# A gated cross-attention and FFN layer: the end of the kernel written in one planned order, with the work spread over engines anew

## The chip, the cores and the metric

The kernel runs on one core of one Trainium2 chip. The core has five engines, each of which works through its own list of instructions in order: TensorE (PE, matmuls), VectorE (DVE), ScalarE (ACT), GpSimd (POOL) and SyncE (SP, which here only issues DMAs). They wait for each other on semaphores. The metric is the device time of one execution in microseconds (us), the median of several; lower is better.

## The reference, cut to what matters

x has 32 batches of 224 tokens of 512 numbers, the context 32 batches of 750 keys of 384 numbers. All is float32.

```python
x = x + tanh(g_xattn) * attention(layernorm(x), ctx, mask, Wq, Wkv)   # 16 heads of 32
x = x + tanh(g_ffn) * ffn(layernorm(x))

def attention(x, y, pad_mask, Wq, Wkv):
    q, (k, v) = x @ Wq.T, split(y @ Wkv.T)
    a = where(pad_mask, (q * scale) @ k.T, -1e9)          # pad_mask is of the queries
    return softmax(a) @ v

def bitlinear(x, w, b):
    xq = act_quant(rmsnorm(x))        # 127 / max|row|, rounded to whole numbers, scaled back
    wq = weight_quant(w)              # w / mean|w|, rounded to -1, 0, 1, scaled back
    return xq @ wq.T + b
ffn = lambda x: bitlinear(gelu(bitlinear(x, w1, b1)), w2, b2)         # 512 -> 2048 -> 512
```

## The kernel before, in words

**Attention.** The main loop (line 915) runs over 128 steps, one for each batch `b` and each group `g` of four heads. In a step `weights` (369) makes, three times, the scores of 250 keys by 224 queries and four heads (`se`), lets ACT take the exponential into a tile `p`, and lets POOL add the two halves of `p` to `acc` (125 x 896; two adds, but for the first of the three, which takes one). There is one PSUM buffer for scores (`ps_s`, used by `sm` and `se` in turn), so PE fills it again only when ACT, or DVE, has emptied it. For the step after it, `maxima` (312) makes scores too (`sm`), which DVE reduces to row maxima (`mx`); `minus_max` splits these into three bfloat16 parts, `turn_max` (358) transposes them on PE and ACT copies the result to `nT`, the first operand of the next `se`. One step later come `values` (402, p by v, 24 matmuls into `po`), `sums` (416, four matmuls of ones by `acc` for the denominators, then a transpose and a reciprocal on DVE), `finish` (432, POOL multiplies) and `store` (441, four DMAs to `o_d` in DRAM).

A step is cut into six slots. Each has its fixed pieces, and what room is left for PE, ACT and DVE is filled by `Ffn.fill` (783).

**Weights.** In steps 0 to 10 the slots 1, 3 and 5 do not take FFN work but one of `weight_units` (451): the FFN weights are loaded twice, first for their mean, then in 16 pieces of 128 x 1024 for `quantise` (490), three passes of DVE over a piece (`wb`, `wb`, then the rounding into `w1q` or `w2q`, fp8).

**FFN.** It goes by pairs of 128 tokens; NF = 28 pairs. `ffn_units` (545) gives a pair's units: `load` (x into `xg`, the attention's result from `o_d` into `og`), `add`, `stats`, `rsqrt` (16 operations on two numbers a row), `norm`, `max`, three `sa`, `grid`, `bias`, `round`, `turn` (two DMA transposes into `xT`); then for each of the two tiles four `b` (4 matmuls `ph`, and DVE scales and adds the bias into `h`), `gelu`, `square`, two `hm` (row maxima), three `sb` (with a second rsqrt, `r3`), `cgrid` (a pass over `h`, 128 x 2048), `cround` (ACT, into `hq`), `cturn` (a DMA transpose into `hT`), two `c` (16 matmuls `po` with `w2q`; DVE adds into `xg`), and `out`. Passes over whole tiles are written for a fixed engine: `add`, `grid`, `bias` and `cgrid` on POOL, `norm`, `round` and `cround` on ACT. Operations on one or two numbers a row go to `small[0]`, which is POOL in the loop and DVE at the end.

Buffers order the units too: `Ffn.behind` (753) lists what a unit comes after. `xg` and `h` have two buffers, `og`, `xc`, `xq`, `xT` and `hq` one.

**What sets the order.** Everything is written through `Ordered` (44), which keeps the written order on each engine. `fill` takes the first ready unit that fits in a slot. `late` (814) gives PE more room, 0.3 us for each tile of backlog beyond `LATE` = 3, or beyond 1 in the last batches. The loop has one step more than there are attention steps, for the last `values`, `sums`, `finish` and `store`. What is left of the FFN is then written by `drain` (819): a list scheduler that takes, at each turn, the ready unit that could begin soonest (within 1.0 us), and among those the one with the longest rest of work behind it. It goes by the table `TAKES_US` (732), in which each unit has one engine.

Of the kernel before, what the change touches and what calls it, by code (L numbers as in the profile page):

```python
# [24 lines left out]
def flamingo_gated_layer(  # L25
# [343 lines left out]
    def weights(b, g, u):  # L369


        qT, kT, nT = q_of[b], k_of[b, g], nT_of[b, g]
        s = ps_s.tile([P, HG, 512], F32, tag="s", name=f"se_{b}_{g}_{u}")
        for j in range(HG):
            pe.matmul(
                s[:KC, j, : 2 * S].rearrange("p (i n) -> p i n", i=2),
                ones3[j * DH : j * DH + 3, :KC],
                nT[j * DH : j * DH + 3, :].unsqueeze(1).to_broadcast([3, 2, S]),
                start=True, stop=False,
            )  # L380
        for i in range(2):
            c = 2 * u + i
            for j in range(HG):
                rows = slice(j * DH, (j + 1) * DH)
                pe.matmul(
                    s[:KC, j, i * S : (i + 1) * S],
                    kT[rows, c * KC : (c + 1) * KC], qT[rows, g, :],
                    start=False, stop=(i == 1),
                )
        p = pp.tile([KC, HG, 2, S], F32, tag="p", name=f"p_{b}_{g}_{u}")  # L390
        act.activation(p.rearrange("p j i n -> p j (i n)"), s[:KC, :, : 2 * S], AF.Exp)
        p_of[b, g, u] = p
        if u == 0:
            acc_of[b, g] = accp.tile([KC, HG, S], F32, tag="acc", name=f"acc_{b}_{g}")
        acc = acc_of[b, g]
        if u == 0:
            gp.tensor_tensor(acc, p[:, :, 0, :], p[:, :, 1, :], ALU.add)
        else:
            for i in range(2):
                gp.tensor_tensor(acc, acc, p[:, :, i, :], ALU.add)  # L400
# [15 lines left out]
    def sums(b, g):  # L416

        po, acc = po_of[b, g], acc_of.pop((b, g))
        for j in range(HG):
            pe.matmul(  # L420
                po[j * DH : (j + 1) * DH, S : 2 * S], ones[:KC, :DH], acc[:, j, :],
                start=True, stop=True,
            )


        oT = op.tile([P, 2, S // DH, DH], F32, tag="oT", name=f"oT_{b}_{g}")
        dve.transpose(oT.rearrange("p a c d -> p (a c d)"), po[:, : 2 * S])
        rd = op.tile([P, S // DH], F32, tag="rd", name=f"rd_{b}_{g}")
        dve.reciprocal(rd, oT[:, 1, :, 0])
        po_of[b, g] = oT, rd  # L430
# [20 lines left out]
    def weight_units():  # L451
# [38 lines left out]
        def quantise(which, i):  # L490
            wl, to = held.pop(("wb", which, i))
            dve.tensor_scalar(wl, wl, wscale[:, which : which + 1], 1.0, ALU.mult, ALU.min)
            dve.tensor_scalar(wl, wl, -1.0, MAGIC, ALU.max, ALU.add)
            dve.tensor_scalar(to, wl, -MAGIC, None, ALU.add, saturate=False)
# [22 lines left out]

    NTI = NT // P
# [25 lines left out]

    def ffn_units(i):
# [6 lines left out]
        def a_load():  # L552
            s["xg"] = xgp.tile([P, TG, D], F32, tag="xg", name=f"xg_{i}")
            s["og"] = ogp.tile([P, TG, D], F32, tag="og", name=f"og_{i}")
            sp.dma_start(
                s["xg"],
                x.rearrange("b s d -> (b s) d")[rows, :].rearrange("(t p) d -> p t d", p=P),
            )
            sp.dma_start(s["og"], o_d[rows, :].rearrange("(t p) d -> p t d", p=P))

        def a_add():
            gp.tensor_tensor(s["xg"], s["xg"], s.pop("og"), ALU.add)
# [17 lines left out]
        def a_norm():  # L580
            s["xc"] = fp.tile([P, TG, D], F32, tag="xc", name=f"xc_{i}")
            for t in range(TG):
                act.activation(
                    s["xc"][:, t, :], s["xg"][:, t, :], AF.Identity, bias=s["nm"][:, t : t + 1]
                )
# [10 lines left out]
        def a_grid():  # L596
            for t in range(TG):
                gp.tensor_scalar(
# [4 lines left out]
        def a_bias():  # L603

            for t in range(TG):
                gp.tensor_tensor(s["xg"][:, t, :], s["xg"][:, t, :], b2g, ALU.add)

        def a_round():
            s["xq"] = fp.tile([P, TG, D], BF16, tag="xq", name=f"xq_{i}")
            act.activation(s["xq"], s["xc"], AF.Identity, bias=magic)  # L610

        def a_turn():
            s["xT"] = fp.tile([P, TG, NDC, P], BF16, tag="xT", name=f"xT_{i}")
# [3 lines left out]
        def b_matmul(t, f):  # L617
            if f == 0:
                s["h", t] = hp.tile([P, F], F32, tag="h", name=f"h_{i}_{t}")
# [14 lines left out]
        def b_gelu(t):  # L634
            h = s["h", t]
            act.activation(h, h, AF.Gelu)
            if small[0] is gp:

                act.activation(warm, magic, AF.Exp)
# [23 lines left out]
        def c_grid(t):  # L663
            h = s["h", t]
            gp.tensor_scalar(h, h, s[f"qb{t}"][0], MAGIC, ALU.mult, ALU.add)

        def c_round(t):
            s["hq", t] = fp.tile([P, F], BF16, tag="hq", name=f"hq_{i}_{t}")
            act.activation(s["hq", t], s.pop(("h", t)), AF.Identity, bias=magic)
# [15 lines left out]
        def c_store(t):  # L685
# [5 lines left out]
            ("add", 3, "load", 0, 0, 0, a_add),  # L691
            ("stats", 2, "add", 0, 0, 1.6, a_stats),
# [38 lines left out]
    ORDER_ONLY = "b", "c"  # L731
    TAKES_US = {
        "load": [("SP", 3.7)], "add": [("POOL", 2.5)], "stats": [("DVE", 1.7)], "rsqrt": [("DVE", 2.6)],
        "norm": [("ACT", 1.4)], "max": [("DVE", 1.2)], "sa0": [("DVE", 0.4)],
        "sa1": [("DVE", 0.2)], "sa2": [("DVE", 0.4)], "grid": [("POOL", 1.4)],
        "bias": [("POOL", 2.5)], "round": [("ACT", 1.2)], "turn": [("SP", 2.7)],
        "b": [("PE", 0.9), ("DVE", 0.75)], "gelu": [("ACT", 1.9)], "square": [("ACT", 2.1)],
        "hm": [("DVE", 1.2)], "sb0": [("DVE", 0.2), ("DVE", 1.8)], "sb1": [("DVE", 0.2)],
        "sb2": [("DVE", 0.4)], "cgrid": [("POOL", 2.0)], "cround": [("ACT", 2.0)],
        "cturn": [("SP", 2.3)], "c": [("PE", 1.75), ("DVE", 0.5)], "out": [("SP", 2.0)],  # L740
    }

    class Ffn:
# [9 lines left out]
        def behind(self, pair, name):  # L753
# [3 lines left out]
                "load": [(pair - XG, f"out{TG - 1}"), (pair - 1, "add")],  # L757
                "norm": [(pair - 1, "round")],
                "round": [(pair - 1, "turn")],
                "turn": [(pair - 1, f"b{TG - 1}3")],  # L760
            }
            if name[-1].isdigit():
# [3 lines left out]
                    f"b{t}0": [(pair, "turn"), (ph, f"cround{th}"), (p1, f"b{t1}3")],  # L766
                    f"square{t}": [(p1, f"square{t1}")],
                    f"sb{t}0": [(pair, f"hm{t}0"), (pair, f"hm{t}1"), (p1, f"sb{t1}2")],
                    f"cround{t}": [(p1, f"cturn{t1}")],
                    f"cturn{t}": [(ph, f"c{th}1")],  # L770
                    f"c{t}0": [(pair, "bias")],
                }
            return [at for at in before.get(name, []) if at[0] >= 0]

        def ready(self, pair, unit):
            name, lag, after = unit[:3]
            if after is not None:
# [36 lines left out]
        def late(self, stored, more):  # L814

            ready = stored * S // P - TG * self.next + sum(p[1][-1][0][:3] == "out" for p in self.parts)
            return 0.3 * max(0, ready - (LATE if stored < B - 3 else 1) - more)

        def drain(self):


            small[0] = dve
            free = dict.fromkeys(("PE", "ACT", "DVE", "POOL", "SP"), 0.0)
            end = {}

            def takes(name):
                kind = name.rstrip("0123456789")
                return TAKES_US.get(kind + name[-1]) or TAKES_US[kind]

            while self.next < NF:  # L830
# [4 lines left out]
            def rank(at):  # L835

                if at not in left:
                    left[at] = 0.0
                    left[at] = sum(us for _, us in takes(at[1])) + max(
# [7 lines left out]
            }  # L847
            while self.parts:
                self.slot += 10
                found = []  # L850
                for part in self.parts:
                    for unit in part[1]:
                        if self.ready(part[0], unit):
                            at = part[0], unit[0]
                            since = max(
                                [end.get(x, 0.0) for x in behind[at]
                                 if x[1].rstrip("0123456789") not in ORDER_ONLY
                                 or x[1][:-1] != at[1][:-1]], default=0.0,
                            )
                            since = max(since, free[takes(unit[0])[0][0]])  # L860
                            found.append((since, -rank(at), part, unit))
                soon = min(f[0] for f in found) + 1.0
                at, _, part, unit = min((f for f in found if f[0] <= soon), key=lambda f: f[1])
                part[1].remove(unit)
                self.at[part[0], unit[0]] = self.slot
                unit[6]()
                for engine, us in takes(unit[0]):
                    at = max(at, free[engine])
                    free[engine] = at + (0.1 if engine == "SP" else us)
                    at += us  # L870
                end[part[0], unit[0]] = at
# [43 lines left out]
    for n in range(N + 1):  # L915
        b, g = steps[n] if n < N else (B, 0)
        nxt = steps[n + 1] if n + 1 < N else None
# [16 lines left out]
        if n < N:  # L934
            put(0, 0.2, lambda: turn_max(n), first=True)
# [7 lines left out]
        if n < N and g == 2 and b + 2 < B:  # L943
# [5 lines left out]
        if n < N:  # L949
            put_values(4)  # L950
        if n < N and g < 2:
            put_values(3, 5)
        more = b + 1 < B and n < N
# [11 lines left out]
        for k in range(6):  # L965
            if k % 2 == 0:
                if nxt:
                    maxima(*nxt, k // 2)
            else:
                if k == 3 and last:  # L970
                    finish(*last)
                if n < N:
                    weights(b, g, k // 2)
            if k == 4 and nxt:
# [17 lines left out]
    ffn.drain()  # L992
# [38 lines left out]
```

## Time and profile before

| | us |
|---|---|
| three runs: median, lowest, highest | 3029.06, 3025.5, 3031.29 |
| the profiled execution, its own time | 3033.95 |
| its span, first to last instruction | 3032.1 |
| PE busy | 2898.3 |
| DVE, ACT, POOL busy | 1754.6, 1403.0, 2081.6 |
| mean granted clock of PE over the span | 0.986 of full |
| last exponential of the attention ends at | 2933.25 |

All times in the trace are from the start of the span. Every instruction is recorded by one helper, so all show line 52, and one goes by the names of tiles: `se` and `sm` are scores, `pk`, `pv` and `pq` projections, `po<-p,v` the attention's values, `ph` and `po<-w2q` the two FFN products. "PE" is matmuls, "PEld" weight loads. A line of the waits reads: who waited, for whom, total us, times, longest.

### The profile page before, as it was taken

The numbers are of one execution on the slowest core, as the hardware profiler recorded it, in microseconds if no ns is written. First come the engines' busy times: TensorE is split into PE (matmuls) and PEld (weight loads), VectorE is DVE, ScalarE is ACT, GpSimd is POOL, SyncE is SP. The second block draws the span as 40 slices with busy tenths as digits, with TensorE's granted clock in tenths as the row PEclk, the third lists the DMA queues.
The fourth block names the chain that finished last, engine by engine and source line by source line (L and its number), as shares of the span: only waits on it lengthen the run. The fifth ranks groups of instructions, "written<-read, shape, count | busy, mean of one in ns | idle before, by whom it ended". The sixth has DMA issues, their size and how long they took to land.

```text
span 3032.1 us, 62700 instructions
## 1 busy us (share of the span) xinstructions
PE 2898.3 (96%) x26774; PEld 1839.4 (61%) x26774; DVE 1754.6 (58%) x2641; ACT 1403.0 (46%) x1396; POOL 2081.6 (69%) x2675
## 2 busy tenths in 40 slices
PE   8998999999999999999999999999999999999964
PEld 4655566566666666666666666666666666666632
DVE  4577565555656556555556556565565555555535
ACT  2332354454545445354354545444543554544543
POOL 3465867768667777776676777766767777767762
PEclk9999999999999999999999999999999999999977
DMA  4333222123222223222222321223222122322112
GB/s 141 93 111 98 52 50 55 48 55 74 59 66 38 63 59 74 66 56 48 51 54 61 73 67 35 63 57 72 56 60 66 28 71 61 73 68 51 25 44 66
DMA packets 352696, 190.02 MB, mean 63 GB/s; under 512 B 282144, under 2 KB 305056, under 8 KB 352288
## 3 DMA queue, kind: packets, MB, share of 16 engines
q1 hardware_dynamic: 352416, 186.01, 25.2%
q8 instruction: 209, 3.42, 0.5%
q14 instruction: 71, 0.58, 0.1%
HBM read 119.86 MB, written 29.39 MB: 49 GB/s over the span
## 4 chain that ended last, share of the span: by engine, by line
PE 79%; ACT 8%; DVE 6%; POOL 4%; DMA 2%; issue 1%; SPq 0%; ACTq 0%; POOLq 0%; DVEq 0%
PE po L52 17%; PE se L52 13%; PE pk L52 13%; PE sm L52 12%; PE pv_None L52 11%; PE ph L52 6%; ACT p L52 6%; DVE mx L52 4%; PE pv L52 4%; PE pq L52 3%; POOL acc L52 2%; POOL h L52 1%; ACT L52 1%; ACT h L52 1%; DMA hT<-hq 1%
## 5 line engine op out<-in xcount | busy, mean ns | idle before, releaser
L52 POOL TENSOR_TENSOR acc<-acc,p 125x896 f32<-125x896 f32 x512 | 1073.2, 2096 | 296.0 <-ACT p L52 274.4
L52 DVE TENSOR_REDUCE mx<-sm 112x4 f32<-112x2000 f32 (+1 forms) x384 | 860.9, 2242 | 597.9 <-PE sm L52 597.6
L52 ACT ACTIVATE p<-se 125x1792 f32<-125x1792 f32 x384 | 639.1, 1664 | 717.7 <-PE se L52 711.3
L52 PE MATMUL pk<-y,wkv_sb 128*128 128x375 f32 x1536 | 545.1, 491 | 9.8 <-DMA y<-in_ctxT 9.8
L52 PE MATMUL sm<-kT,qT 32*112 32x500 f32 (+1 forms) x4096 | 427.2, 509 | 27.3 <-ACT p L52 17.7
L52 POOL TENSOR_TENSOR acc<-p 125x896 f32<-125x896 f32 x128 | 268.5, 2098 | 247.3 <-ACT p L52 247.3
L52 PEld LDWEIGHTS pk<-y,wkv_sb 128*128 128x128 f32 x1536 | 277.7, 191 | 179.6 <-issue 43.2
L52 PE MATMUL pv_None<-wkv_sb,y 128*125 128x256 f32 x1548 | 367.9, 387 | 0.0
L52 PE MATMUL se<-qT,kT 32*125 32x224 f32 x6144 | 360.2, 349 | 0.0
L52 PEld LDWEIGHTS pv_None<-wkv_sb,y 128*125 128x125 f32 x1548 | 280.1, 187 | 130.7 <-issue 88.3
L52 PE MATMUL po<-p,v 125*32 125x224 f32 x6144 | 319.2, 356 | 0.0
L52 PEld LDWEIGHTS se<-qT,kT 32*125 32x125 f32 x6144 | 295.9, 183 | 0.0
L52 PEld LDWEIGHTS sm<-kT,qT 32*112 32x112 f32 x4096 | 159.5, 171 | 186.1 <-ACT p L52 120.8
L52 ACT COPY kT<-pk 128x375 f32<-128x375 f32 x256 | 120.1, 469 | 318.0 <-PE pk L52 317.6
L52 DVE SCALAR_TENSOR_TENSOR h<-ph,qa_am,b_sb 128x512 f32<-128x512 f32 x224 | 165.3, 747 | 169.3 <-PE ph L52 147.1
L52 PEld LDWEIGHTS po<-p,v 125*32 125x32 f32 x6144 | 187.2, 110 | 119.9 <-issue 44.4
L52 PE MATMUL ph<-w1q,xT 128*128 128x512 fp8e4 x896 | 227.5, 388 | 23.2 <-DMA xT<-xq 22.9
L52 PE MATMUL po<-w2q,hT 128*128 128x256 fp8e4 x1792 | 219.5, 277 | 26.1 <-DMA hT<-hq 26.1
L52 PE MATMUL pq<-xTb,wq_sb 128*128 128x224 f32 x1024 | 221.1, 359 | 1.1 <-DVE wq_sb L52 0.7
L52 PEld LDWEIGHTS <-hT 128*128 128x128 bf16 x1792 | 170.7, 99 | 68.5 <-DMA hT<-hq 28.0
L52 PEld LDWEIGHTS pq<-xTb,wq_sb 128*128 128x128 f32 x1024 | 186.9, 190 | 25.4 <-issue 16.9
L52 POOL TENSOR_TENSOR yo<-oT,rd 128x224 f32<-128x224 f32 x128 | 73.7, 576 | 184.3 <-DVE rd L52 117.9
(119 smaller groups left out, 2914.3 us busy)
## 6 DMA issues: line engine op xcount, KB each, us to landing
y<-in_ctxT SPq DMA_DIRECT2D x31, 1125.0 KB, 6.9
x<-in_x SPq DMA_DIRECT2D x32, 448.0 KB, 7.7
xTb<-in_xT SPq DMA_DIRECT2D x32, 448.0 KB, 3.9
o_d<-yo SPq DMA_DIRECT2D x512, 28.0 KB, 1.6
xg<-in_x SPq DMA_DIRECT2D x28, 512.0 KB, 3.7
og<-o_d SPq DMA_DIRECT2D x28, 512.0 KB, 4.6
out<-xg SPq DMA_DIRECT2D x56, 256.0 KB, 2.1
wa<-in_w1T SPq DMA_DIRECT2D x8, 512.0 KB, 7.3
```

The lines of the kernel that those rows point to most:

```text
L52: return lambda *args, **kw: tc.keep_in_program_order(build(*args, **kw))
```

## The change

- **Last step.** The loop's extra step goes, and the last step is no longer in the loop either. Its `turn_max`, three `weights`, and the last two steps' `values` and `sums`, `finish` and `store` are handed to `drain` as units beside the FFN's. A `gelu` in the drain comes after the last `weights`. In the last step POOL no longer adds the two halves of the last third into `acc`; PE sums them with eight more matmuls of ones.
- **Engines.** In the drain a unit may have several ways in `TAKES_US` (`add`, `grid`, `bias` and `cgrid` on POOL or DVE, `norm`, `round` and `cround` on ACT or DVE, the small operations on DVE or POOL); the planner takes the way that ends first, with 1 us added for each us of DVE. `small[0]` is set for each unit. SP's entries have the time of their queue apart, and the window is 2 us.
- **Homes.** The last two pairs have no tiles of their own kind: x and the attention's result go into a `y` tile, `xc` and `xq` into a `v` tile, `xT` into a `kT` tile, `hq` into `x` tiles, and the hidden tiles of the last pair but one into the projection weights `wq_sb` and `wkv_sb`. Their entries in `behind` shrink accordingly. The last pair loads x at once, and fetches the attention's result after the last `store`.
- **Held back.** `late` takes 3 in the last batches, where it took 1 (and the bounds of "last" move).
- **Weights.** The third pass of `quantise` goes from DVE to ACT.

```diff
-        else:
+        elif (b, g, u) != (*steps[-1], 2):
             for i in range(2):
                 gp.tensor_tensor(acc, acc, p[:, :, i, :], ALU.add)
...
+        parts = [acc]
+        if (b, g) == steps[-1]:
+            parts += [p_of[b, g, 2][:, :, i, :] for i in range(2)]
+        for i, part in enumerate(parts):
+            for j in range(HG):
+                pe.matmul(
+                    po[j * DH : (j + 1) * DH, S : 2 * S], ones[:KC, :DH], part[:, j, :],
+                    start=(i == 0), stop=(i == len(parts) - 1),
+                )
...
-            dve.tensor_scalar(to, wl, -MAGIC, None, ALU.add, saturate=False)
+            act.activation(to, wl, AF.Identity, bias=magic, saturate=False)
...
+    def rounded(to, of):
+        if small[0] is dve:
+            dve.tensor_scalar(to, of, -MAGIC, None, ALU.add)
+        else:
+            act.activation(to, of, AF.Identity, bias=magic)
...
+            if i >= NF - 2:
+                both = yp.tile([P, NYC * M], F32, tag="y", name=f"xo_{i}")
+                both = both[:, : 2 * TG * D].rearrange("p (a t d) -> p a t d", a=2, t=TG)
+                s["xg"], s["og"] = both[:, 0], both[:, 1]
...
-            gp.tensor_tensor(s["xg"], s["xg"], s.pop("og"), ALU.add)
+            small[0].tensor_tensor(s["xg"], s["xg"], s.pop("og"), ALU.add)
...
-            gp.tensor_scalar(h, h, s[f"qb{t}"][0], MAGIC, ALU.mult, ALU.add)
+            small[0].tensor_scalar(h, h, s[f"qb{t}"][0], MAGIC, ALU.mult, ALU.add)
...
-            return 0.3 * max(0, ready - (LATE if stored < B - 3 else 1) - more)
+            return 0.3 * max(0, ready - (LATE if stored < B - 8 else 3) - more)
...
-            small[0] = dve
-            free = dict.fromkeys(("PE", "ACT", "DVE", "POOL", "SP"), 0.0)
+            draining.append(True)
+            free = {"PE": 0.0, "ACT": 0.0, "DVE": 4.3, "POOL": 5.0, "SP": 0.0}
...
+                            way = min(
+                                takes(unit[0]), key=lambda way: course(at, way)[1]
+                                + 1.0 * sum(us for engine, us in way if engine == "DVE"),
                             )
...
+                small[0] = {"DVE": dve, "POOL": gp}.get(way[-1][0], act)
                 unit[6]()
...
-    ffn.drain()
+    last = steps[-2:]
+    ffn.drain(
+        [("top", 0, None, 0, 0, 0, lambda: turn_max(N - 1))]
+        + [(f"w{u}", 0, None, 0, 0, 0, lambda u=u: weights(*last[1], u)) for u in range(3)]
+        + [
+            (name, 0, None, 0, 0, 0, lambda do=do, at=at: [f(*at) for f in do])
+            for name, at, *do in (
+                ("val", last[0], values, sums), ("fin0", last[0], finish), ("sto0", last[0], store),
+                ("vlast", last[1], values, sums), ("fin1", last[1], finish), ("sto1", last[1], store),
+            )
+        ]
+    )
```

## The prediction

> **What bounds the kernel now.** I read the page first, then five windows over the end, then the chain of waits and the totals of waits there, then the stretch in which the weights are quantised.
>
> ```profile
> PE 2898.3 (96%) x26774; PEld 1839.4 (61%) x26774; DVE 1754.6 (58%) x2641; ACT 1403.0 (46%) x1396; POOL 2081.6 (69%) x2675
> PE   8998999999999999999999999999999999999964
> PEclk9999999999999999999999999999999999999977
> ```
>
> TensorE is busy in 96% of the span, at a granted clock of nine tenths or more, except at both ends. In the middle only taking TensorE work away helps; what else can be won lies in the first slices and in the last two.
>
> ```profile
> 2846.00:2899.00 53.00, 49.16 (x458) 29.38 (x460) 25.93 (x37) 20.13 (x22) 36.88 (x37) 0.94 0.22 51
> 2899.00:2933.00 34.00, 21.01 (x266) 12.01 (x258) 17.04 (x28) 24.99 (x20) 26.23 (x46) 0.85 0.03 6
> 2933.00:2960.00 27.00, 14.42 (x120) 10.00 (x120) 4.15 (x9) 3.48 (x4) 13.95 (x17) 0.69 0.31 67
> 2960.00:2996.00 36.00, 15.46 (x54) 6.24 (x55) 23.33 (x71) 14.52 (x12) 12.57 (x10) 0.67 0.25 59
> 2996.00:3032.10 36.10, 19.00 (x141) 13.99 (x138) 16.87 (x45) 13.72 (x9) 4.54 (x3) 0.85 0.31 73
> ```
>
> Columns: stretch, length, busy time of PE, weight loads, DVE, ACT, POOL, then clock, DMA share, GB/s. The last exponential ends at 2933.25 (call this instant E). From E to the end, 98.9 us, PE works 48.9, DVE 44.4, ACT 31.7 and POOL 31.1: no engine is the bound; they take turns. The chain shows why:
>
> ```profile
> 2945.12 2.01 ACT hq L52
> 2947.15 4.27 DMA hT<-hq
> 2951.46 6.24 PE po L52 x32
> 2957.73 0.48 DVE xg L52
> 2958.21 0.09 DVE qa_c L52
> ...
> 2961.83 4.21 DMA xT<-xq
> 2966.09 5.75 PE ph L52 x16
> ```
>
> One tile is rounded, turned and multiplied before DVE gets to the reciprocal of the next pair, since that stands behind `xg<-po` in DVE's order. The totals from 2899 on say the same of DVE, and show one hole before E:
>
> ```profile
> DVE xg L52 <- PE po L52: 34.2, 11, 9.9
> ...
> PE se L52 <- ACT nT L52: 6.4, 1, 6.4
> ```
>
> The last pair's rsqrt starts only at E+39.4 (2972.62), its last transposed input lands at E+56.5 (2989.7), the last transposed hidden tile at E+91.7 (3024.95).
>
> **Part 1, the rounding of the weights (16 passes, DVE to ACT).** DVE's timeline of that stretch, and what PE waits for from 175 to 300:
>
> ```profile
> 198.18 2.46 DVE L52 TENSOR_SCALAR wb<-wb 128x1024 f32<-128x1024 f32 x1
> 200.67 2.58 DVE L52 TENSOR_SCALAR w1q<-wb 128x1024 fp8e4<-128x1024 f32 x1
> ...
> 213.84 0.69 DVE L52 TENSOR_SCALAR wb<-wb 128x1024 f32<-128x1024 f32 x1
> 214.57 0.70 DVE L52 TENSOR_SCALAR w1q<-wb 128x1024 fp8e4<-128x1024 f32 x1
> ```
> ```profile
> PE se L52 <- DVE mx L52: 9.9, 11, 3.6
> ```
>
> The same pass takes 0.69 us alone and 2.46 to 2.58 where a POOL `acc` runs beside it. Taking the third pass away gives DVE 5 x 2.55 + 11 x 0.70 = 20.4 us, but PE can gain only what it waited for: the gain lies between 0 and 9.9. By single holes of PE in front of `se`: four of 0.77 behind the slow passes go (3.1), one of 1.92 behind a 2.45 third pass goes nearly whole (1.8), one of 3.54 is a wait for a weight load and shrinks by the pass of 0.70. Sum 5.6. ACT takes 16 passes; the nearest row is `xq`, 128x1024, 1.15 us, 18.4 in all, and ACT is busy 4 to 5 us in 15 here. Each stands just behind an exponential, and behind it a copy of `kT` or `v`. If instead each delayed an exponential by its 1.15, PE would lose up to 18; I take 5.6 as gain.
>
> **Part 2, work held back.** The instruction order shows that behind the last exponential 24 groups of `ph` and 14 of `po` with `w2q` now stand, where 16 and 12 stood. A group of four `ph` takes PE 0.865 us from start to start, one of sixteen `po` 1.75. So 8 x 0.865 + 2 x 1.75 = 10.4 us leave the stretch where PE is the bound. The hole of 6.4, a gelu with two table loads (1.28 each) ahead of `nT`, goes, since gelu now waits for the last weights; but the new order has an `hq` (2.0), which waits for POOL's pass over `h` (1.97) behind two `acc`, ahead of that `nT`: about 4.5. Such a hole also halves the clock for a while: after 2888 eight `ph` took 3.59 instead of 1.90 and the sixteen `se` 1.81 instead of 0.93, some 3 us in all. I let the two holes cancel and charge 3 for one more half-clock stretch. E moves by 5.6 + 10.4 - 3 = 13 us. If nothing is charged it is 16, if the hole comes out as two, 9.
>
> **Part 3, from E to the end.** I walked the new order, each unit starting when its engine is free and its inputs are there, with these rows (us): `acc` 2.09, bn stats and aggregate 0.85 per tile, small operations on POOL 0.20 to 0.35 plus 0.08 between them, `h<-ph` 0.75, `hm` 1.20, gelu and square 1.91 and 2.1, `hq` 2.0, POOL `h` 1.97, turns 1.25 + 2.65 for `xT` and 4.29 for `hT`, `og` 4.64, stores of `o_d` 1.9 of issuing + 1.6. Not in the trace: DVE's add of 128x1024. Its nearest row from below is the `amax` reduction of as many elements, 1.20 (both one element at a time); POOL's add took 2.36. I take 1.2. DVE's passes over 128x512, 128x1024 and 128x2048 are scaled from 0.74 for 1024 elements. The path of the last pair:
>
> - to E+5.0: two `acc` (the other two of the last third are gone), then twelve `po` sums, which carry the dropped adds on PE for about 1.2 where four took 0.5
> - to E+10.9: DVE is held 4.4 us by passes and an `amax` of other pairs; then transpose 0.65, reciprocal 0.2, `yo` 0.56
> - to E+20.9: store 3.2, `og` 4.7, DVE still in `xg` 0.9, add 1.2
> - to E+27.2: stats 1.8, POOL's rsqrt of sixteen small operations 4.4
> - to E+38.4: DVE in `h<-ph` and `hm` of two other pairs 4.5, `amax` 1.2, scales 1.3, `hm` again 2.7, grid and rounding 1.5
> - to E+47.0: two turns 3.9, four `ph` groups with `h` 4.7
> - to E+59.7: ACT finishes an `hq`, then two gelu, two squares and a wait for the second `h`; POOL still has a pass over the pair before (2.0) and its scales
> - to E+72.5: POOL's two `r3` chains of 3.5, scales, DVE held 1.8 by `xg<-po`, pass over `h` 2.0
> - to E+83: `hq` 2.0, turn 4.3, two `po` groups and `xg` 4.2
> - to E+86.1: store and end 3.1, as before
>
> In this walk DVE works 55 us (44 in the old windows) and POOL 46 (31). Two things are added. Nine of DVE's SBUF-only passes meet POOL; the quantise rows say nothing to 1.9 for one. The two with small POOL operations beside them cost about 0.3, and most of the others sit on the path; I take 3.8, ends 0 and 17. And the clock: it is granted at 0.67 to 0.85 in the three old windows, and eight `ph` groups and four `po` groups of the path at half clock for a part cost 2 (ends 0 and 8). E+92.
>
> On that first term a rule speaks against the change. By the Trainium skill (SBUF — State Buffer, Who interferes with whom) a DVE `tensor_scalar` on both ports and a POOL instruction exclude each other, and the one that comes second is blocked for the whole of the other. Here two `acc` in a row from 194.16, 4.24 together elsewhere, took 5.93, because a DVE pass that came second, at 197.40, ran its 0.74 in the middle of them; only the DVE pass after it waited. By the rule alone each of the seven passes that meet a long POOL operation waits for its rest, an estimate of 1 us each, 7 in all.
>
> The last pairs in homes of their own cost nothing themselves: the tiles they take are dead by then. What they remove is visible: the old load of the last `xg` was issued at 2960.30, right after `out<-xg` at 2958.24.
>
> **Sum.** Own span 3032.1 - 13 - (98.9 - 92) = 3012; the execution took 3033.95, so 3014 for it; the median of the runs shown is 3029.06, 4.9 lower. The same 20 us off that: 3009.
>
> **Rivals.**
> - *Appended, not overlapped:* the 10.4 us that leave the loop come back in full behind E because every engine's order is still a string of turns (E+109.3). Then only part 1 and the clock remain: 3029 - 5.6 + 3, about 3026, within 0.2%. For it: no engine was over half busy behind E and still it took 98.9. Against: the last pair's rsqrt moves from E+39.4 to E+22.8. 7%.
> - *Ports:* all nine DVE passes wait 1.9, 17 instead of 3.8: 3022. Between that and my value lies 3015 to 3022. 13%.
> - *No charges:* holes, ports and clock cost nothing: 16 + 12.8 off, 3000; with part 1 at its upper end 2996. 10%.
> - *DVE's order becomes the bound, slower:* DVE waits at the head of its queue for every PE group. Old waits: 34.2/11 = 3.1 per `xg<-po`, 4.5/5 = 0.9 per `h<-ph`. With 14 and 24 groups that is 43.5 + 21.6 on 55 of work and 4 before: E+124, so 13 earlier and 25 later, 3041. It is slower than before when these waits exceed about 53. Against: the walk has some 25. 5%.
>
> **Chances.** The forecast's own case (3002 to 3015) holds 65%. This kernel's measurement tells 0.2%, 6 us, from no change. Faster by more: 65 + 10 + 13 and little of the first rival, 0.88; within: 0.07; slower: 0.05. The range runs from 2998 to 3020: it leaves out the appended case, the slow one, and the ends of two others.
>
> **What would show it.** Part 1: from 175 to 300 the wait of `se` for `mx` falls from 9.9 to some 4, and the exponentials there run 5 us earlier by 300. Part 2: E near 2920, no `nT` wait of 6.4 behind a gelu. Part 3: about 92 us behind E, the last pair's first rsqrt step 23 to 26 us after E, DVE's wait for `po` below 34.2 in spite of more groups. Wrong, if DVE passes of 0.74 show up at over 2 us on the path, if PE's clock stays at a half through the end, or if exponentials from 175 to 300 wait for ACT.

## The result, and the profile after

| | before | after |
|---|---|---|
| median of six runs each (lowest to highest), us | 3029.01 (3025.5 to 3031.29) | 3012.09 (3009.68 to 3013.2) |
| profiled execution: own time, span | 3033.95, 3032.1 | 3009.68, 3007.9 |
| end of the last exponential, E | 2933.25 | 2920.4 |
| from E to the end of the span | 98.9 | 87.5 |

The changed kernel takes 0.9943 of the time before (95% interval 0.993 to 0.9956), 17 us less. The two profiles lie 24 apart, since that of before is 4.9 above its median and that of after is the fastest of its six runs.

The page of after, busy times and the two rows of PE in 40 slices:

```profile
PE 2896.7 (96%) x26790; PEld 1840.5 (61%) x26790; DVE 1735.9 (58%) x2574; ACT 1409.6 (47%) x1401; POOL 2087.6 (69%) x2729
PE   8999999999999999999999999999999999999976
PEclk9999999999999999999999999999999999999978
```

PE has the same work; its last slice but one rises from 6 to 7 and its last from 4 to 6. Five windows over the end of after (columns as before; E lies at the end of the second):

```profile
2846.00:2886.00 40.00, 33.93 (x352) 20.91 (x344) 24.34 (x37) 19.10 (x19) 29.11 (x45) 0.95 0.21 53
2886.00:2920.60 34.60, 23.13 (x255) 14.34 (x252) 10.97 (x22) 13.47 (x11) 27.19 (x38) 0.66 0.16 35
2920.60:2948.00 27.40, 21.82 (x153) 10.54 (x151) 21.52 (x30) 10.26 (x10) 15.33 (x37) 0.88 0.25 57
2948.00:2984.00 36.00, 17.45 (x105) 10.36 (x104) 28.52 (x46) 23.37 (x16) 23.97 (x57) 0.82 0.33 59
2984.00:3007.90 23.90, 17.69 (x127) 13.77 (x124) 5.35 (x12) 4.00 (x2) 7.46 (x18) 0.84 0.50 121
```

Behind E PE is busy 57.0 of 87.3 us, where it was 48.9 of 98.9: more of its work is done there, in less time. In the 27 us just behind E DVE went from 4.15 to 21.52. What the engines wait for stands in the totals of waits from 2886 on (who, for whom, total us, times, longest):

```profile
PE ph L52 <- DMA xT<-xc: 15.3, 2, 12.1
DVE xo L52 <- PE po L52: 14.7, 8, 5.3
...
ACT hq L52 <- POOL h L52: 12.7, 3, 7.5
DVE oT L52 <- PE po L52: 11.0, 2, 9.0
```

The waits of DVE for `po` into `xo` are shorter than those into `xg` were (34.2 in all, the longest 9.9), and PE's longest in the list is for a transposed input. The chain of waits over the same stretch (start, length, engine and tile):

```profile
2964.82 1.98 POOL h L52
2966.83 2.00 ACT hq L52
2968.86 4.51 DMA hT<-hq
2973.42 1.93 PE po L52 x16
...
2983.41 7.70 PE po L52 x48
...
2996.45 4.26 DMA hT<-hq
3000.75 3.68 PE po L52 x32
```

The chain still goes from engine to engine at the end (pass, rounding, turn, product), but the 48 matmuls of `po` from 2983.41 belong to more than one tile (a tile has 32) and run without a pause: other pairs' work now lies beside the last one's.

### The profile page after: what moved, and what is told of

Read it like the earlier page. It is cut to its first block, busy times and chain, and to the rows that moved or that the text cites. A ratio compares the mean times of both kernels' runs of the same rounds, so it can differ in the third digit from the quotient of the medians.

```text
span 3007.9 us, 62728 instructions
## 1 busy us (share of the span) xinstructions
PE 2896.7 (96%) x26790; PEld 1840.5 (61%) x26790; DVE 1735.9 (58%) x2574; ACT 1409.6 (47%) x1401; POOL 2087.6 (69%) x2729
## 4 chain that ended last, share of the span: by engine, by line
PE 80%; ACT 8%; DVE 5%; POOL 3%; DMA 3%; issue 1%; SPq 0%; POOLq 0%; ACTq 0%; DVEq 0%
PE po L52 17%; PE se L52 13%; PE pk L52 13%; PE sm L52 12%; PE pv_None L52 10%; PE ph L52 6%; ACT p L52 5%; PE pq L52 4%; PE pv L52 4%; DVE mx L52 4%; POOL acc L52 2%; ACT L52 1%; ACT h L52 1%; PE pn L52 1%; DMA r_d<-ve 0%
## 5 line engine op out<-in xcount | busy, mean ns | idle before, releaser
L52 PEld LDWEIGHTS pv_None<-wkv_sb,y 128*125 128x125 f32 x1548 | 280.2, 187 | 130.6 <-issue 89.8
L52 ACT COPY v<-pv_None 125x512 f32<-125x512 f32 x96 | 56.2, 585 | 308.9 <-PE pv_None L52 308.9
```

Of the source, the lines that this page charges most:

```text
L52: return lambda *args, **kw: tc.keep_in_program_order(build(*args, **kw))
```

## The experiments

Theory: each of the three parts pays as in the sum (cast 5.6, held work some 7, the end 7), and the end pays because each engine's order there is no longer a string of turns. Rivals: the work held back only moves behind E; the cast is lost again later; one small thing of the list (a home, a second way, the planner's numbers) carries the whole gain.

Each ratio is to the kernel before, measured beside it (its median there: 3029.98 for the first four, 3030.22 for the next four, 3029.06 for the last four). E and the stretch behind E are of one profiled execution each, with 3032.1 - 98.9 for before.

| | median (runs) | ratio, 95% interval | E | behind E |
|---|---|---|---|---|
| e1_only_cast | 3027.14 (11) | 0.9992 (0.9984 to 1.0001) | 2928.1 | 98.0 |
| e2_only_held | 3038.65 (7) | 1.0029 (1.0018 to 1.004) | 2928.3 | 108.9 |
| e3_not_held | 3013.64 (5) | 0.9948 (0.9935 to 0.996) | 2926.9 | 87.1 |
| e4_one_way | 3019.17 (5) | 0.9965 (0.9952 to 0.9979) | 2922.1 | 95.3 |
| e5_changed_again | 3012.61 (5) | 0.9943 (0.993 to 0.9955) | 2923.1 | 89.8 |
| e6_not_held_again | 3015.31 (5) | 0.9947 (0.9935 to 0.996) | 2928.4 | 86.9 |
| e7_cast_back | 3015.81 (5) | 0.9951 (0.9938 to 0.9963) | 2927.5 | 86.8 |
| e8_replanned | 3007.29 (5) | 0.9926 (0.9913 to 0.994) | 2919.2 | 86.3 |
| e9_no_homes | 3030.45 (11) | 1.0005 (0.9996 to 1.0014) | 2923.7 | 103.7 |
| e10_home_of_x_only | 3008.33 (5) | 0.994 (0.9927 to 0.9953) | 2923.0 | 87.7 |
| e11_no_dve_pass | 3014.64 (5) | 0.9959 (0.9946 to 0.9972) | 2920.5 | 90.4 |
| e12_replanned_again | 3010.92 (5) | 0.9943 (0.9929 to 0.9957) | 2922.2 | 87.0 |

**The cast.** Alone on the kernel before (e1), and taken out of the changed one (e7):

```diff
-            dve.tensor_scalar(to, wl, -MAGIC, None, ALU.add, saturate=False)
+            act.activation(to, wl, AF.Identity, bias=magic, saturate=False)
```

> The kernel before with one edit: the third pass of quantise goes to ACT. Theory (the pass leaves DVE's way to the row maxima, and ACT has room behind each exponential): 5 to 6 us less than before, all of it between 170 and 300 us, with the wait of se for mx in that stretch down from 9.9 to about 5, and nothing changed behind the last exponential. Rival (ACT's pass waits for DVE and holds the exponential behind it): no gain, or up to 18 us more, with se or sm waiting for ACT p by more than the 1.6 of before.

> The changed kernel with the third pass of quantise back on DVE. Theory: 4 to 6 us more than the changed kernel, the wait of se for mx from 174 to 299 at 8 to 10 again, all else alike. Rival (the pass was hidden, the 5 us seen by 346 us are given back later): within 2 us.

Alone it gives 3029.98 - 3027.14 = 2.8, with an interval that just takes in nothing; taken out it costs 3015.81 - 3012.61 = 3.2. Both are some half of what was expected, though 0.9984 leaves room for 4.8. The trace shows where a part goes: in e1 the exponentials are 5.2 us earlier than in the profile of before at 346 us and 5.3 at 484, but 2.6 at 940 and 2.2 at 2298. Over the eleven profiles with the cast (after and ten experiments) the mean lead at 2298 is 4.2 (from 2.2 to 5.9); those without it, e2 and e7, stand at -0.4 and -0.1. Of the 4.2, 1.4 stood already at 80 us, ahead of the first weight pass, so 2.8 were won behind that, which is what the medians show. The last section tells a part of what happens between 484 and 940.

**The held work.** Alone on the kernel before (e2), and taken out of the changed one, twice (e3, e6):

```diff
-            return 0.3 * max(0, ready - (LATE if stored < B - 3 else 1) - more)
+            return 0.3 * max(0, ready - (LATE if stored < B - 8 else 3) - more)
```

> The kernel before with one edit: late takes 3 in the last batches, so one more pair is left for the end, under the old planner. Theory (what leaves the loop is only worth something if the end overlaps it; under the old planner the end is a string of turns): the last exponential 4 to 10 us earlier, the stretch behind it about 10 longer, in sum 0 to 5 us more than before. Rival (the relief of PE in the loop is the gain, whatever stands at the end): 7 to 10 us less than before.

> The changed kernel with one part undone: late takes 1 again in the last batches. Theory (under the new planner the work held back lies beside other work): the last exponential some 5 us later than in the changed kernel, the stretch behind it no shorter or by 2 us at most, in sum 5 to 7 us more than the changed kernel, so 10 to 12 less than before. Rival (held work is appended here too): the stretch behind it shorter by what the loop got longer, in sum as the changed kernel.

> The changed kernel with late at 1 in the last batches, again, now beside the changed kernel. The two profiles so far put its last exponential 6.5 us later and the stretch behind that equally long, the medians of different calls only 1.5 apart. Theory (under the new planner the held work lies beside other work): 4 to 7 us more than the changed kernel. Rival (appended): within 2 us of it.

Under the old planner E moves up by 4.9 and the stretch behind it grows by 10.0: 8.7 us slower in the medians, more than any theory had. Two rows of its waits from 2928 to the end:

```profile
PE ph L52 <- DMA xT<-xq: 24.0, 2, 15.7
...
POOL xc L52 <- DVE qa_c L52: 18.4, 1, 18.4
```

They are no shorter than in the kernel before (22.9 and 14.2), and behind E PE stands idle for some 56 us, where it was 50: the work held back fills no hole, and the rival that it is only appended holds there. In the changed kernel the same `late` moves E by 5.9 (2921.7, mean of after and e5, against 2927.6 of e3 and e6) and lengthens the rest by 1.7 (88.7 against 87.0); PE's idle time behind E is 30 and 32 us with the held work (after, e5), 42 and 39 without it (e3, e6), so there it does fill holes. So 4 us should be left; the medians show 1.2 to 2.7 (by the ratios 0.0004 to 0.0005, so 1.2 to 1.5; against e5, measured beside it, 2.7), less than the theory and, in e3, within the rival's 2. The intervals overlap almost wholly, so the medians don't tell it from nothing. Some 2 of the 4 us are the choice of executions: the profiled ones of e3 and e6 lie 2.1 and 1.8 above their medians, those of after and e5 2.4 below and 2.1 above.

**The planner's ways.** One way for each unit, as in the old table (e4); then only the passes over whole tiles bound to POOL and ACT, with the small operations free (e11):

```diff
-        "add": [[("DVE", 1.2)], [("POOL", 2.4)]], "stats": [[("DVE", 1.7)]],
-        "rsqrt": [[("DVE", 2.6)], [("POOL", 3.2)]],
+        "add": [[("POOL", 2.4)]], "stats": [[("DVE", 1.7)]],
+        "rsqrt": [[("DVE", 2.6)]],
...
-        "sb2": [[("DVE", 0.4)], [("POOL", 0.6)]], "cgrid": [[("DVE", 1.7)], [("POOL", 2.0)]],
-        "cround": [[("ACT", 2.0)], [("DVE", 1.8)]], "cturn": [[("SP", 3.8)]],
+        "sb2": [[("DVE", 0.4)]], "cgrid": [[("POOL", 2.0)]],
+        "cround": [[("ACT", 2.0)]], "cturn": [[("SP", 3.8)]],
```

> The changed kernel with one part undone: every unit of the drain has one engine again (add, grid, bias and cgrid on POOL, norm, round and cround on ACT, small operations on DVE). Theory (with one engine for each pass DVE carries all rsqrt chains and the turns come back): the last exponential as in the changed kernel, the stretch behind it 6 to 9 us longer, so the whole 6 to 9 more than the changed kernel. Rival (DVE's passes and POOL block each other, so spreading brings nothing): the stretch is as long or shorter, and no DVE pass of a plain 0.7 us takes more than 1 us.

> The changed kernel with add, grid, bias and cgrid on POOL alone and norm, round and cround on ACT alone; the small operations still go to DVE or POOL as the planner likes. In the profile of the changed kernel four groups of DVE passes took 1.76, 1.88, 1.75 and 2.34 beside POOL where 0.74 was costed, 4.8 us in all. Theory (the passes are still worth it, since they take work off POOL and ACT on the path): 2 to 6 us more than the changed kernel. Rival (ports): 1 to 5 us less.

e4 costs 0.0022 of the time, 6.7 us, as the theory had it (each of its runs is slower than every run of after and e5), and all of it lies behind E (95.3 against 87.5 and 89.8). Its waits from 2922 on show DVE as the one that the others stand for:

```profile
POOL wq_sb L52 <- DVE qb_c L52: 15.8, 1, 15.8
...
POOL h L52 <- DVE qb_c L52: 13.5, 2, 12.2
```

POOL stood idle until DVE came to the scales, operations on one or two numbers a row; behind E it works 28 us there, against 47 in after. e11 may give back part of that: it is 4.5 us faster than e4 by the medians and 1.8 by the ratios, and 2.5 slower than the changed kernel by the medians and 4.8 by the ratios. All these intervals overlap, so how the 6.7 divide between the second way of the small operations and the passes on DVE isn't shown.

**The homes.** Taken away from the last two pairs, so that they use the pools and wait as the other pairs do (e9; the last step's second scores then come after `val`). Then only the home of x and the attention's result given back (e10):

```diff
-            if i >= NF - 2:
+            if i >= NF:
                 both = yp.tile([P, NYC * M], F32, tag="y", name=f"xo_{i}")
...
-                "load": [(pair - XG, f"out{TG - 1}"), (pair - 1, "add")],
-                "fetch": [(NF, "sto1")],
+                "load": [(pair - XG, f"out{t}") for t in range(TG)] + [(pair - 1, "add")],
+                "fetch": [(NF, "sto1"), (pair - 1, "add")],
```

> The changed kernel with one part undone: the last two pairs use the pools' own tiles, with the waits that go with them (load after both out of the pair two before, and so on); and the planner is told that the second weights come after the first val, which the changed kernel does anyhow. Theory (the last pair's early start is the root of the gain at the end): the last pair's first rsqrt step 35 us or more behind the last exponential instead of 22, the stretch behind it 12 to 20 us longer, the whole 12 to 20 more than the changed kernel, so within 6 of before. Rival (the planner and the ways do it, the homes are a convenience): at most 4 us more than the changed kernel.

> The changed kernel with only x and the attention's result of the last two pairs in a home of their own; xc, xq, xT, h and hq are in the pools' tiles again. Theory (what matters is that the load is not behind out): within 3 us of the changed kernel. Rival (every shared tile strings the pairs together): half or more of what the kernel without any homes loses.

Without homes the whole gain is gone: 1.0005. E is still early (2923.7), but 103.7 us follow it. SP's queue of e9 shows the load of the last pair where it was in the kernel before, behind the store of the pair that held its buffer:

```profile
2959.88 0.36 SPq L52 DMA_DIRECT2D out<-xg  x1
2961.93 0.40 SPq L52 DMA_DIRECT2D xg<-in_x  x1
```

and of after:

```profile
2908.01 1.13 SPq L52 DMA_DIRECT2D xo<-in_x  x1
```

That is 38 us behind E in e9 and 12 us ahead of it in after. But the load isn't the last thing that the pair waits for in e9. Its `add` waits for the attention's result, `og`, which SP fetches behind the load and a turn:

```profile
2966.14 0.45 SPq L52 DMA_DIRECT2D og<-o_d  x1
2970.26 2.35 POOL L52 TENSOR_TENSOR xg<-xg,og 128x1024 f32<-128x1024 f32 x1 [5.56 <-DMA og<-o_d]
```

The last store that this fetch needs is late as well: it begins at 2955.01, in after at 2929.43. With the one home given back, which holds both x and the attention's result, the load goes at 2910.92 and the kernel is as fast as the changed one (0.994 against 0.9943), with the tiles `xc`, `xq`, `xT`, `h` and `hq` back in their pools. In e10 the last pair's first rsqrt step comes at E+30.6, against 21.6 in after and 51.5 in e9, and the stretch is 87.7: ten us later at that step cost nothing, thirty cost sixteen. So the home of both inputs is what pays; what the early load of x is worth without the rest was not run. And e9 keeps the work held back, which alone, without homes, costs 8.7 (e2): a part of the 18 us that e9 loses may be that, and no run leaves out both.

**The changed kernel once more, and other numbers for the planner** (e5; e8; e12, which also binds `round` to ACT, lets POOL begin at 8 and weighs DVE by 1.2):

```diff
-        "turn": [[("SP", 2.6)]], "b": [[("PE", 0.9), ("DVE", 0.75)]],
+        "turn": [[("SP", 4.0)]], "b": [[("PE", 0.9), ("DVE", 0.75)]],
...
-            free = {"PE": 0.0, "ACT": 0.0, "DVE": 4.3, "POOL": 5.0, "SP": 0.0}
+            free = {"PE": 0.0, "ACT": 0.0, "DVE": 3, "POOL": 6, "SP": 0.0}
...
-                                + 1.0 * sum(us for engine, us in way if engine == "DVE"),
+                                + 0.8 * sum(us for engine, us in way if engine == "DVE"),
...
-                soon = min(f[0] for f in found) + 2
+                soon = min(f[0] for f in found) + 1.5
```

> The changed kernel itself, a second time, so that the three beside it have it on their own chip and a second profile of it exists. Theory: 16 to 18 us less than before, and a profile whose exponentials are 5 to 7 us ahead of the old ones by 346 us and 11 to 13 by the last one; its clock dips of 3.41 or 6.83 us may fall elsewhere and move it by 2 to 3. If instead the last exponential is ahead by less than 9, the first profile flattered the change.

> The changed kernel with four numbers of the planner put nearer to the trace: turn 4.0 instead of 2.6 (two transposes land 3.9 after the first issue), DVE free at 3 and POOL at 6, the extra for DVE 0.8, the window 1.5. The order behind the last exponential changes, the work does not. Theory (the stretch is set by who stands where in each engine's order, so better numbers find a shorter one): 1 to 4 us less than the changed kernel. Rival (such numbers only shuffle the order): anywhere from 5 less to 10 more.

> The changed kernel with other numbers for the planner: turn 4.0, round on ACT alone, POOL free at 8, the extra for DVE 1.2, the window 1.5. Theory (numbers nearer to the trace shorten the stretch, as in the first kernel replanned): 2 to 6 us less than the changed kernel. Rival (the first one was a lucky order): no better than the changed kernel.

e5 repeats the ratio, 0.9943, though its profile ends 5.0 later than that of after. e8 is 5.3 faster than e5, measured beside it, more than the theory's 1 to 4, though the intervals just overlap; e12, made on the same idea with the turn at its measured length too, has the changed kernel's ratio. So the gain of e8 is that of one order that came out well, not shown to be that of truer numbers.

## Why the prediction was right, point by point

The sum was 20 us off the median (5.6 for the cast, 7.4 more up to E, 6.9 behind E); it came out as 17. That it came so near is in part luck: the cast left some 3 of its 5.6, and the stretch behind E got shorter by 9.1 to 11.4 where the sum had 6.9. For the terms there are two profiles of the changed kernel, after and e5, and one of before.

- **What bounds the kernel:** right. PE's busy time hardly changes (2898.3 and 2896.7), and what was won lies in the first slices and in the last two.
- **Part 1, the mis-sized term.** In the trace it is as predicted: from 174 to 299 the wait of `se` for `mx` is 5.2 (predicted about 4, from 9.9), as in the other kernels with the cast (5.0 to 5.8; 8.3 and 9.5 in two without it), and the exponentials are 5 us earlier there. PE waits 1.6 for `p` in both kernels, so no exponential is late on ACT's account. The row:

```profile
PE se L52 <- DVE mx L52: 5.2, 7, 4.0
```

  But the lead does not last: in after it is 6.9 at 484 us and 5.9 at 2298, in e5 5.7 and 2.6, in the mean of eleven profiles 4.2 there, of which 1.4 stood at 80 us already, and the medians give 2.8 to 3.2. The prediction took what PE gains at 300 us as what is left at the end.
- **Part 2, E.** Predicted 13 in all; 12.8 in after, 10.2 in e5 (11 to 13 were expected of it). The part beyond the lead of the first stretch is 6.9 and 7.6, where 7.4 were predicted. Its parts are also near: the `nT` wait is 3.7 (about 4.5 predicted), and PE runs longer at half clock, 0.66 in the window before E. That E moves was the point; the price behind E, that of more work there, is 1.7 with homes and ways (after and e5 against e3 and e6) and 10.0 without (e2). The rival "appended" is true of this edit alone; in the changed kernel the traces speak against it, while the medians (1.2 to 2.7) don't decide.
- **Part 3, behind E.** Predicted 92, measured 87.5 and 89.8. The last pair's first rsqrt step comes at E+21.6 (E+23 to 26 predicted), the last transposed hidden tile lands at 3000.70, E+80.3 (in e5 at E+82.6); the walk had it at E+78.8 (83 less the 4.2 behind it), to which its 5.8 of charges come. So the walk was nearly right by itself, and of the 5.8 charged on it 1.5 came on the path in after and 3.8 in e5. The DVE passes that meet POOL are there, though:

```profile
2922.75 1.76 DVE L52 TENSOR_SCALAR xq<-xc 128x1024 bf16<-128x1024 f32 x1 [7.32 <-DMA o_d<-yo]
2924.44 1.88 DVE L52 TENSOR_SCALAR xc<-xo,nm 128x512 f32<-128x512 f32 x2
...
2938.99 1.23 DVE L52 TENSOR_TENSOR xo<-xo 128x1024 f32<-128x1024 f32 x1
...
2955.61 2.34 DVE L52 TENSOR_SCALAR xc<-xc,qa_c 128x512 f32<-128x512 f32 x2
```

  With one at 2936.27 of 1.75 and 0.74 for a pass of 1024 elements alone, these make 1.02 + 1.14 + 1.60 + 1.01 = 4.8, where 3.8 were charged. The add that no row showed took 1.23 (1.2 taken). The Trainium skill (SBUF — State Buffer, Who interferes with whom) has the second one blocked for the whole of the first, which was estimated at 1 us a pass. Four of the passes agree with that in size. POOL lost too: its two `xg` additions beside the first of them took 2.95, where they take 2.54 alone. e11, with no such pass on DVE, is not faster (2.5 slower by the medians, with overlapping intervals), so no run shows that these waits cost more than the second engine brought.
- **The homes.** "Cost nothing themselves" was right, and said too little: the load that no longer stands behind `out` was named as what they remove, but in the sum it had no price. e9 prices the homes: without them the rest of the change, the held work with it, gives nothing (1.0005). e10 shows that one of the five does it, that of x and the attention's result. A walk without it would have shown the last pair's rsqrt some 30 us later, and been the most telling bound of the forecast.
- **The other rivals.** DVE's order did not become the bound: its waits for `po` are 14.7 for `xo` and 11.0 for `oT`, against 34.2 for `xg` and 7.1 for `oT` in before. Nor did all charges vanish: a half clock before E and the meeting passes are in the trace. That the end pays by work shared between engines holds (e4), but without the homes the whole gains nothing (e9).
- **From profile to median.** The two profiles of the changed kernel lie 24.2 and 19.2 below that of before (spans), 21.7 in the mean; 4.9 of that is the one execution of before that was profiled, and 21.7 - 4.9 = 16.8 is what the medians show. The prediction took its 20 off the median as if none of the 4.9 lay in the stretches that the change shortens. In which of them it lies can't be told from one profile of before.

What stays open: why e8's order is better than e12's, and whether its order with only the home of x is better still (not run); what the home of x and the attention's result gives the kernel before by itself, or a kernel without the held work (not run). Undone one at a time, the parts weigh 3.2 for the cast, 1.2 to 2.7 for the held work, 6.7 for the ways and 18 for the homes; that is more than the 17 in all, so the parts lean on each other. The held work shows it most: 8.7 lost by itself (e2), nothing lost beside homes and ways.

## What to carry to other kernels

At the end of a kernel look first for the inputs of the last tile: if they wait for a buffer that an earlier tile gives back late, a better order behind them may bring nothing, as here, and a dead tile of another stage is a free home for them. Work moved from the loop behind the loop can pay only if the engines there are free to take it beside the rest; try that move alone and it may cost, as here, 8.7 us. And where a change saves single microseconds early in a long kernel, measure it in many runs: its lead in one trace is not yet its gain.

## What the runs showed of the hardware

In the records of granted clock PE falls to half speed for pieces of 3.4 us or a multiple of it (3.4, 6.8, 10.2, 13.7), and the pieces lie on a grid that begins elsewhere in each execution. A hole of PE ahead of one `se`, from 505.37 in after and from 506.49 in e5, is 1.81 us long in both; the window of 505 to 515 of after, and then of e5, the same program:

```profile
505.00:515.00 10.00, 8.19 (x116) 5.07 (x118) 5.01 (x3) 2.61 (x3) 7.61 (x19) 1.00 0.43 65
```

```profile
505.00:515.00 10.00, 8.19 (x67) 4.61 (x69) 3.87 (x6) 3.18 (x6) 8.72 (x19) 0.83 0.48 65
```

The clock is 1.00 in one and 0.83 in the other (half of it for 3.4 us), with the same hole. What differs is where the grid cuts it. In e5 the piece of the grid ahead of the dip holds the whole hole, and PE is busy for less than half of that piece (columns as before):

```profile
505.20:508.60 3.40, 1.59 (x13) 0.74 (x15) 3.01 (x4) 0.84 (x3) 3.32 (x3) 1.00 1.02 103
508.60:512.00 3.40, 3.40 (x23) 2.10 (x16) 0.00 (x0) 1.66 (x1) 2.50 (x13) 0.50 0.38 85
```

In after the next dip, at 554.4, puts a bound of the grid at 506.6 (14 pieces back), inside the hole; 1.25 us of idle time lie in the piece ahead of it, 0.6 in the one behind. So it is in all fourteen profiles: from 400 to 700 us every piece in which PE is idle for 1.79 us or more is followed by one at half clock (21 of them), and none in which it is idle for 1.71 or less. Over the whole of 90 to 2850 us, some 11,270 pieces at full clock, two don't fit: one of 1.93 that no half clock follows, and one of 1.55 that it does.

In e5 the lead falls by 2.7 from 484 to 940 us, in after by 0.5. The dip at this hole is in the profiles of e1 to e5, e8 and e9, where the lead falls by 1.6 to 2.9 there; it is not in those of after, e6, e7 and e10 to e12 (0 to 1.6), nor in that of before; so 1.6 can be lost there without it too (e11). The Trainium skill (TensorE: Matmul & The Clock Gate, What's actually happening) tells of a free-running window of about 3.4 us and of run-to-run differences at the start of a kernel. The lengths agree with it; but its advice (Why this matters for your kernels) to keep holes below about 3 us is not enough here, as one of 1.81 us is followed by a dip wherever it lies whole in one piece of the grid. Such dips, and a start that varies by some 3 us (at 80 us the profiles stand from 0.4 behind that of before to 2.5 ahead of it), may make up the 10 us between the runs of one kernel; only the profiled runs have a trace, so it isn't shown. Nor is it shown that the cast makes the dip more frequent (six of eleven profiles with it, one of three without): the hole, 1.79 to 1.81 us long, is in all fourteen, and only the grid lies elsewhere.
